# The gated activations of a decoder layer: transposed by VectorE in 32x32 squares instead of by TensorE

## The chip, the cores and the metric

The kernel runs on one core of a Trainium2 chip. The metric is device time in microseconds (us). Before the change it is 2656.92 us, the median of three runs (2655.61 to 2657.28). The engines are called by short names: PE is TensorE, DVE is VectorE, ACT is ScalarE, POOL is GpSimd, and SP is the engine whose queue issues most of the DMAs. PEld is the weight-load side of PE.

## The reference

The reference is one decoder layer on x of shape 16 x 112 x 1024 (1792 tokens) in float32. It has three blocks, each followed by a residual sum and a layer norm. Cut to the first block, which the change touches:

```python
s = silu(x @ w_gate.T)                 # 1792 x 2752
_, idx = top_k(-abs(s), 1376)          # the smaller half of each row ...
s[row, idx] = 0.0                      # ... is set to zero
h = s * (x @ w_up.T)
x = layernorm(x + h @ w_down.T)
```

The second block is cross attention over a context of 16 x 375 x 1024 (32 query heads, 8 key heads of 32), the third a linear layer with 4-bit weights. Neither is changed.

## The kernel before

The tokens are 14 tiles of 128. The work runs in stages on PE, one after the other.

- **Gates** (5.9 to 526 us): per tile six chunks of about 456 columns, eight products each (line 146). The results go through ACT and DVE to the DRAM buffer s_d.
- **Keys and values** (526 to 853 us): lines 176 and 184.
- **Up** (853 to 1403 us): per tile six chunks, 512, 512 and 352 columns twice, eight products each (line 234).
- **Down** (1405 to about 1890 us): h times w_down by a seven-product scheme over 2 x 2 blocks (line 546), with layer norm behind it.
- **Attention and the last layer**: the rest.

Beside the first three stages ACT and DVE look for the threshold of each row, which decides what is set to zero. For each tile there are 31 steps; in a step ACT counts over 1824 columns (line 284) and DVE over 928 (line 287), then DVE updates the candidate (lines 295 and 296). Two tiles are searched in turns. When a tile's search ends, `finish` adds twelve pieces: eight on DVE (lines 314 to 343), four on POOL (lines 347 and 348), and the mask goes to m_d. The function `beside`, called after each half step, takes one such piece and then emits chunks of the stream until it has emitted `share` columns more: the sum of the stream's weighted widths over 448 half steps. An up chunk is weighted 1.07 times its width.

Everything between is in the order in which it is written, on every engine: `as_written` ties each instruction to the one before it on its engine. So an instruction that waits holds all that is behind it on that engine, and a DMA that waits holds the DMAs behind it in the same queue.

An up chunk n goes through these steps. `emit` first calls `turn` for a chunk three back. Then `up_chunk(n)` calls `load_up(n + 1)`: on SP the tile's input uxT if chunk n + 1 is the first of a tile (line 138), then that chunk's s and mask (lines 211 and 212), and on POOL s times mask (line 213). Then come the eight products into a PSUM bank. Then `settle` emits the evacuation of the chunk before: DVE multiplies s by the product in PSUM (line 241), which gives h, 128 tokens on partitions. `turn` makes h transposed: PE transposes each 128 columns (line 255) into one of two PSUM banks, ACT copies them to the tile hT (lines 257 and 261), and POOL's queue stores hT in the DRAM buffer hT_d of that token tile (lines 258 and 262). The stream's products have the six other banks.

The down stage loads blocks of hT_d on SP (`block`, lines 532 and 533), 128 rows of h by 128 tokens for each of 11 parts, the last with 96 rows. Each part is the stationary operand of one product (`product`, line 546). DVE adds and subtracts whole blocks (`combine`, lines 553 and 554).

Of the kernel before, what the change touches and what calls it, by code (L numbers as in the profile page):

```python
# [10 lines left out]
F32 = mybir.dt.float32  # L11
# [6 lines left out]
ALU = mybir.AluOpType  # L18
AX = mybir.AxisListType
PSUM = bass.MemoryType.PSUM  # L20
DRAM = bass.MemoryType.DRAM

P = 128
B, S, D = 16, 112, 1024
NT = B * S
TT = NT // P
# [4 lines left out]
Q = 32  # L31
NKQ = -(-SK // Q)
SKP = NKQ * Q
NKP = -(-SK // P)
NH, NKV, HD = 32, 8, 32
REP = NH // NKV
KVD = NKV * HD
# [8 lines left out]
FH = FF // 2  # L46
UP_CHUNKS = [(h * FH + o, w) for h in range(2) for o, w in ((0, 512), (512, 512), (1024, 352))]
HK = -(-FH // P)
FULL, REST = FH // P, FH % P
# [48 lines left out]


def gates_keys_up(  # L100
    nc, tc, ident, xT, wg, wu, ctxT, wk, wv, s_d, m_d, hT_d, k_d, v_d, down, left, ps_g, ps_t
):


# [14 lines left out]
    io = io_ctx.enter_context(tc.tile_pool(name="g_io", bufs=2, side="right"))  # L119
# [103 lines left out]
    def up_chunk(n):  # L223
        t, c = ups[n]
        off, w = UP_CHUNKS[c]
        if n == 0:
            load_up(0)
            for tag, many, bufs in (("wk", 4, 1), ("wv", 4, 1), ("ctx", 6, 2), ("ctx", 6, 2)):
                to_load.extend(down.place(kvp, tag, many, bufs))
        load_up(n + 1)  # L230
        load_down()
        pu = ps_g.tile([P, 512], F32, tag="pg", name=f"pu_{t}_{c}")
        for kc in range(KC):
            nc.tensor.matmul(  # L234
                pu[:, :w], xts[t][:, kc, :], wu_sb[0][:, kc, ds(off, w)],
                start=(kc == 0), stop=(kc == KC - 1),
            )

        def evacuate():
            s = sm[t, c]  # L240
            nc.vector.tensor_mul(s[:, :w], s[:, :w], pu[:, :w])

        return evacuate

    def turn(n):

        t, c = ups[n]
        off, w = UP_CHUNKS[c]
        h = sm.pop((t, c))
        k0, nk = off // FH * HK + off % FH // P, -(-w // P)  # L250
        pt = ps_t.tile([P, 4, P], F32, tag="pt", name=f"pt_{t}_{c}")
        hT = io.tile([P, 4, P], F32, tag="hT", name=f"hT_{t}_{c}", bufs=2)
        for k in range(nk):
            r = min(P, w - k * P)
            nc.tensor.transpose(pt[:r, k, :], h[:, ds(k * P, r)], ident)  # L255
        whole = w // P
        nc.scalar.copy(hT[:, :whole, :], pt[:, :whole, :])
        nc.gpsimd.dma_start(hT_d[t][:, k0 : k0 + whole, :], hT[:, :whole, :])
        if nk > whole:
            r = w % P  # L260
            nc.scalar.copy(hT[:r, whole, :], pt[:r, whole, :])
            nc.gpsimd.dma_start(hT_d[t][:r, k0 + whole, :], hT[:r, whole, :])

    state = {}

# [100 lines left out]
    stream = deque()  # L366
# [6 lines left out]
    for b in range(B):  # L373
        for u in range(2 + NKP):
            stream.append((SK if u < 2 else KVD, lambda b=b, u=u: kv_unit(b, u)))
    for n, (t, c) in enumerate(ups):
        stream.append((UP_CHUNKS[c][1] * 1.07, lambda n=n: up_chunk(n)))
    found, pieces = set(), deque()


# [90 lines left out]
class Down:  # L471
# [54 lines left out]
    def block(self, t, h):  # L526

        pool = (self.a1, self.a2)[self.n_blocks // 4 % 2] if self.a2 else self.a1
        self.n_blocks += 1
        a = pool.tile([P, HK, P], F32, tag="h", name=f"h_{self.n_blocks}", bufs=4)  # L530
        h_d = self.hT_d[t]
        self.nc.sync.dma_start(a[:, :FULL, :], h_d[:, ds(h * HK, FULL), :])
        self.nc.sync.dma_start(a[:REST, FULL, :], h_d[:REST, h * HK + FULL, :])
        return a

    def first_blocks(self):
# [6 lines left out]
    def product(self, bank, a, b):  # L543
        for k in range(HK):
            r = P if k < FULL else REST
            self.nc.tensor.matmul(  # L546
                bank, a[:r, k, :], b(k)[:r],
                start=(k == 0), stop=(k == HK - 1),
            )

# [85 lines left out]
    def load_sums(self, j):  # L636

        v = self.nc.vector
        a11, a12, a21, a22 = (self.block(2 * j + i, h) for i in range(2) for h in range(2))
        self.combine(v, a22, a21, a22, ALU.add)  # L640
        self.combine(v, a21, a11, a21, ALU.subtract)
        self.combine(v, a22, a22, a11, ALU.subtract)
        self.combine(v, a12, a12, a22, ALU.subtract)
        self.live[j] = a22, a21, a12

    def load_rest(self, j):

        a21, a22 = (self.block(2 * j + 1, h) for h in range(2))
        self.combine(self.nc.vector, a21, a21, a22, ALU.add)
        self.live[j] = a21, a22  # L650

    def last_pass(self, beside):
# [119 lines left out]
def attention_and_ffn(nc, tc, ident, ident_b, negh, x1_d, k_d, v_d, queries, wf_sb, wo, out):  # L772
# [16 lines left out]
    with ExitStack() as ctx:  # L789
# [23 lines left out]
        def load_values(b, c):  # L813
            vals[b, c] = ld.tile([P, NKP, P], F32, tag="v", name=f"v_{b}_{c}")
            nc.sync.dma_start(
# [304 lines left out]
@with_exitstack  # L1120
def kernel(
    ctx: ExitStack,
    tc: tile.TileContext,
    x: bass.AP,
    xT: bass.AP,
    ctxT: bass.AP,
    wg: bass.AP,
    wu: bass.AP,
    wd: bass.AP,
    wq: bass.AP,  # L1130
    wk: bass.AP,
    wv: bass.AP,
    wo: bass.AP,
    qw: bass.AP,
    qs: bass.AP,
    qz: bass.AP,
    out: bass.AP,
):
    nc = tc.nc
    const = ctx.enter_context(tc.tile_pool(name="const", bufs=1))  # L1140
    dram = ctx.enter_context(tc.tile_pool(name="dram", bufs=1, space=DRAM))
    ident = const.tile([P, P], F32, tag="ident", name="ident")
    make_identity(nc, ident)
    ident_b = const.tile([P, P], BF16, tag="ident_b", name="ident_b")
    nc.vector.tensor_copy(ident_b, ident)
    negh = const.tile([P, 1], F32, tag="negh", name="negh")
    nc.gpsimd.memset(negh, -0.5)

    s_d = [dram.tile([P, FF], F32, tag=f"s{t}", name=f"s_d{t}") for t in range(TT)]
    m_d = [dram.tile([P, FF], BF16, tag=f"m{t}", name=f"m_d{t}") for t in range(TT)]  # L1150
    k_d = dram.tile([B, P, 2, SK], F32, tag="k", name="k_d")
    v_d = dram.tile([B, SKP, KVD], F32, tag="v", name="v_d")
    x1_d = dram.tile([NT, D], F32, tag="x1", name="x1_d")

    hT_d = [dram.tile([P, 2 * HK, P], F32, tag=f"h{t}", name=f"hT_d{t}") for t in range(TT)]
    with as_written(nc, tc):
        with ExitStack() as psum:
            ps_g = psum.enter_context(tc.tile_pool(name="ps_g", bufs=6, space=PSUM))
            ps_t = psum.enter_context(tc.tile_pool(name="ps_t", bufs=2, space=PSUM))
            with ExitStack() as left:  # L1160
                down = Down(nc, tc, negh, wd, hT_d, x, x1_d, ps_g)
                gates_keys_up(
                    nc, tc, ident, xT, wg, wu, ctxT, wk, wv, s_d, m_d, hT_d, k_d, v_d, down, left,
                    ps_g, ps_t,
                )
                down.first_passes()
                a_w = ctx.enter_context(tc.tile_pool(name="a_w", bufs=1, side="right"))
                wq_sb = a_w.tile([P, KC, D], F32, tag="wq", name="wq_sb")
                wf_sb = a_w.tile([P, 8, D], BF16, tag="wf", name="wf_sb")
                queries = Queries(nc, tc, ctx, ident, x1_d, wq_sb, lambda: down.bank("pq"))  # L1170
                with tc.tile_pool(name="q", bufs=2, side="right") as q_pool:

                    def load_wq(i):
                        nc.scalar.dma_start(wq_sb[:, :, ts(i, D // 4)], wq[:, :, ts(i, D // 4)])

                    loads, computes = unpack_steps(nc, q_pool, wf_sb, qw, qs, qz)
                    beside = [[] for _ in range(TT // 2)]
                    for i, j in enumerate((1, 1, 2, 3, 4, 4, 5, 6)):
                        beside[j].append(computes[i])
                    for i, j in enumerate((0, 0, 1, 1, 2, 3, 4, 4)):  # L1180
                        beside[j].append(loads[i])
                    for i in range(4):
                        beside[i // 2].append(lambda i=i: load_wq(i))
                    beside[4].append(lambda: queries.fetch(0, 0))
                    beside[5] += [lambda: queries.rows(0, 0), lambda: queries.fetch(0, 1)]
                    beside[6].append(lambda: queries.rows(0, 1))
                    down.last_pass(beside)
            for mc in range(EARLY):
                queries.chunk(0, mc)
        attention_and_ffn(nc, tc, ident, ident_b, negh, x1_d, k_d, v_d, queries, wf_sb, wo, out)  # L1190
# [48 lines left out]
```

## Time and profile before

| | before |
|---|---|
| median of three runs | 2656.92 us |
| the profiled execution | 2661.48 us |
| its span, first to last instruction | 2659.7 us |
| mean granted TensorE clock | 0.983 |
| PE busy | 2584.9 us (97%) |
| DVE busy | 1730.8 us (65%) |
| ACT busy | 1377.6 us (52%) |
| POOL busy | 1053.8 us (40%) |
| line 234, products of the up stage | 530.6 us, 1344 records |
| line 255, transposes by PE | 44.2 + 7.6 us, 308 records |
| lines 257 and 261, copies by ACT | 50.0 us, 112 |
| lines 258 and 262, stores by POOL | 112 issues |
| line 241, multiplies by DVE | 52.5 us, 84 |
| line 546, products of the down stage | 1078 |

The profile page shows busy time by engine, the span in 40 slices (a digit is the busy share in tenths), and the chain of work that ended last. A line of the timeline or of the chain begins with the start and the length in us. A group's line ends with busy time and mean ns of one, then the idle time of the engine ahead of it and what ended it. A line of waits names who waited, for whom, the total in us, how often, and the longest. The products are pipelined, so a record of a product is longer than the step from one to the next: 16 records of a 512-column chunk take 6.87 us on the chain, 0.43 us each, where a record shows 592 ns.

### The profile page before, as it was taken

How to read it: one execution, taken by the hardware profiler on the slowest of the kernel's cores; microseconds unless marked ns; L12 is line 12 of the kernel's file. 1: busy time of each engine (PE TensorE's matmuls, PEld its weight loads, DVE VectorE, ACT ScalarE, POOL GpSimd, SP SyncE). 2: the span in 40 equal slices, each digit the busy share in tenths (PEclk: the TensorE clock that was granted, in tenths of full speed). 3: DMA queues.
4: the chain of work that ended last, by engine and by line, in shares of the span. 5: the costliest groups of instructions: out<-in, count | busy, mean ns of one | idle time of the engine just before them, and what ended most of it. 6: DMA issues, size and time to landing. Idle time of an engine off the chain costs nothing.

```text
span 2659.7 us, 33179 instructions
## 1 busy us (share of the span) xinstructions
PE 2584.9 (97%) x10266; PEld 1482.7 (56%) x10266; DVE 1730.8 (65%) x3579; ACT 1377.6 (52%) x2413; POOL 1053.8 (40%) x1097
## 2 busy tenths in 40 slices
PE   9999999999999999999999999998899999999997
PEld 4444444577776555555554444443556666667663
DVE  0478778866876788788730343158467777777773
ACT  0487787777767777787610000000255555565553
POOL 0002022213322444344450000023277888788783
PEclk9999999999999999999999999999889999999998
DMA  6221223154443543443346222166567777777763
GB/s 253 94 74 56 77 91 126 51 195 168 181 169 136 162 140 121 143 132 117 95 145 228 86 96 94 59 204 202 133 169 196 196 191 193 192 205 194 188 175 103
DMA packets 216960, 387.70 MB, mean 146 GB/s; under 512 B 32080, under 2 KB 151120, under 8 KB 212688
## 3 DMA queue, kind: packets, MB, share of 16 engines
q1 hardware_dynamic: 165456, 257.19, 32.3%
q0 software_dynamic: 35840, 100.59, 11.6%
q10 hardware_dynamic: 15488, 27.80, 3.5%
q8 instruction: 83, 1.36, 0.2%
q14 instruction: 93, 0.76, 0.1%
HBM read 208.36 MB, written 76.43 MB: 107 GB/s over the span
## 4 chain that ended last, share of the span: by engine, by line
PE 90%; DVE 3%; DMA 3%; ACT 2%; issue 1%; POOL 1%; ACTq 0%; SPq 0%; POOLq 0%; DVEq 0%
PE pg L146 20%; PE pu L234 19%; PE m L546 14%; PE bank L924 7%; PE pk L184 6%; PE pk L176 6%; PE bank L765 6%; PE sc L832 4%; PE po L887 3%; PE bank L975 2%; PE pt L255 1%; ACT probs L840 1%; DVE b L727 1%; DMA xr<-x_d 1%; DVE nmax L838 1%
## 5 line engine op out<-in xcount | busy, mean ns | idle before, releaser
L284 ACT ACTIVATE ja<-a,cand 128x1824 int8<-128x1824 f32 x434 | 788.6, 1817 | 178.4 <-DVE cand L296 174.4
L287 DVE TENSOR_SCALAR_CACHE_REDUCE jv<-a,cand 128x928 uint8<-128x928 f32 x434 | 510.0, 1175 | 56.9 <-ACT a L271 48.8
L234 PE MATMUL pu<-wu_sb,uxT 128*128 128x512 f32 (+1 forms) x1344 | 530.6, 548 | 0.0
L146 PE MATMUL pg<-wg_sb,gxT 128*128 128x456 f32 (+1 forms) x1344 | 519.9, 550 | 5.9 <-DMA wg_sb<-in_wg_dram 5.9
L840 ACT ACTIVATE probs<-sc,nmax 128x375 f32<-128x375 f32 x512 | 287.4, 573 | 237.6 <-DVE nmax L838 218.2
L146 PEld LDWEIGHTS pg<-wg_sb,gxT 128*128 128x128 f32 x1344 | 256.2, 191 | 268.8 <-issue 265.3
L849 POOL TENSOR_TENSOR probs<-probs,sums 128x1500 f32<-128x1500 f32 x128 | 344.2, 2689 | 142.4 <-DVE sums L848 123.2
L234 PEld LDWEIGHTS pu<-wu_sb,uxT 128*128 128x128 f32 x1344 | 249.0, 190 | 230.0 <-issue 188.4
L838 DVE TENSOR_REDUCE nmax<-sc 128x2 f32<-128x750 f32 x256 | 228.6, 932 | 150.3 <-PE sc L832 150.2
L546 PE MATMUL m<-wd,h 128*128 128x512 f32 (+1 forms) x616 | 268.0, 597 | 0.0
L860 DVE STREAM_TRANSPOSE squares<-probs 128x1536 f32<-128x1536 f32 x128 | 224.0, 1750 | 9.7 <-DMA weights<-squares 5.5
L155 POOL DMA_DIRECT2D s_d<-s x84 | 46.0, 548 | 427.4 <-DVE s L154 351.5
L765 PE MATMUL bank<-x1T,wq_sb 128*128 128x224 f32 x976 | 202.6, 361 | 0.0
L546 PEld LDWEIGHTS m<-wd,h 128*128 128x128 f32 (+1 forms) x616 | 117.5, 191 | 149.2 <-issue 145.1
L765 PEld LDWEIGHTS bank<-x1T,wq_sb 128*128 128x128 f32 x976 | 181.3, 191 | 33.2 <-issue 30.2
L924 PE MATMUL bank<-wo_sb,aT 128*128 128x256 f32 x832 | 195.0, 388 | 0.0
L758 ACT COPY x1T<-pq 128x448 f32<-128x448 f32 x4 | 2.0, 535 | 371.6 <-PE pq L757 371.6
L874 POOL DMA_DIRECT2D weights<-squares x320 | 178.6, 564 | 9.0 <-issue 6.6
L924 PEld LDWEIGHTS bank<-wo_sb,aT 128*128 128x128 f32 x832 | 155.4, 192 | 46.5 <-issue 24.9
L184 PE MATMUL pk<-wv_sb,ctx 128*128 128x256 f32 (+1 forms) x768 | 168.4, 379 | 0.0
L176 PE MATMUL pk<-ctx,wk_sb 128*128 128x375 f32 x512 | 164.4, 478 | 0.0
L184 PEld LDWEIGHTS pk<-wv_sb,ctx 128*128 128x128 f32 (+1 forms) x768 | 144.0, 188 | 24.8
(118 smaller groups left out, 2881.8 us busy)
## 6 DMA issues: line engine op xcount, KB each, us to landing
weights<-squares SPq DMA_DIRECT2D x704, 96.0 KB, 3.3
h<-hT_d SPq DMA_DIRECT2D x56, 640.0 KB, 4.5
weights<-squares POOLq DMA_DIRECT2D x320, 96.0 KB, 3.4
ctx<-in_ctxT_dram SPq DMA_DIRECT2D x16, 1500.0 KB, 6.7
a<-s_d SPq DMA_DIRECT2D x14, 1376.0 KB, 7.9
us<-s_d SPq DMA_DIRECT2D x56, 256.0 KB, 2.7
hT_d<-hT POOLq DMA_DIRECT2D x56, 256.0 KB, 3.1
s_d<-s POOLq DMA_DIRECT2D x56, 228.0 KB, 2.2
```

The costliest lines, as they stand in the source:

```text
L146: nc.tensor.matmul(pg[:, :w], xts[t][:, kc, :], wg_sb[:, kc, ds(off, w)], start=(kc == 0), stop=(kc == KC - 1),)
L176: nc.tensor.matmul(pk[:, :SK], wk_sb[:, kc, ts(u, P)], c[:, kc, :], start=(kc == 0), stop=(kc == KC - 1),)
L184: nc.tensor.matmul(pk[:n, :KVD], c[:, kc, ds(at, n)], wv_sb[:, kc, :], start=(kc == 0), stop=(kc == KC - 1),)
L234: nc.tensor.matmul(pu[:, :w], xts[t][:, kc, :], wu_sb[0][:, kc, ds(off, w)], start=(kc == 0), stop=(kc == KC - 1),)
L284: nc.scalar.activation(ja, a[:, NV:], AF.Sign, bias=cand, scale=-1.0, accum_out=st["sgn"])
L287: nc.vector.tensor_scalar(jv, a[:, :NV], cand, -(TOPK - 1 - NA / 2), ALU.is_lt, ALU.add, accum_out=st["nlt"])
L546: self.nc.tensor.matmul(bank, a[:r, k, :], b(k)[:r], start=(k == 0), stop=(k == HK - 1),)
L765: nc.tensor.matmul(pq[:, :GT], self.wq_sb[:, kc, ts(mc, P)], self.x1T[g][:, kc, :], start=(kc == 0), stop=(kc == KC - 1),)
L838: nc.vector.tensor_reduce(nmax[h], sc[h][:, :, :SK], AX.X, ALU.max, negate=True)
L840: nc.scalar.activation(pr[:, i, :SK], sc[i // 2][:, i % 2, :SK], AF.Exp, bias=nmax[i // 2][:, i % 2 : i % 2 + 1], accum_out=sums[:, i : i ...
L849: nc.gpsimd.tensor_tensor(pr, pr, sums.unsqueeze(2).to_broadcast([P, 4, SK]), ALU.mult)
L924: nc.tensor.matmul(pp[:, :256], aT[:, h, r, :], wo_sb[:, h * REP + r, ts(i, 256)], start=(h == 0 and r == 0), stop=(h == 1 and r == REP - 1),)
```

## The change

`turn` no longer uses PE, ACT or the two PSUM banks. DVE transposes each chunk of h in squares of 32 x 32 from SBUF to SBUF. A square's transpose stays on its 32 partitions, so the block is not yet in order: the 32 tokens of group b lie on partitions 32 b to 32 b + 31. Four stores a chunk, one for each group, put it together in hT_d; two go on SP's queue and two on POOL's. Within a chunk the rows k of the four 128-column parts are innermost, so a row of 32 tokens by four parts is 512 bytes in DRAM (three parts and 384 bytes for the 352-column chunk, of which the missing 32 rows are set to zero by POOL).

The down stage loads a block in one transfer of 128 partitions. A part's stationary operand is now every fourth (third) word of it. The blocks' sums are made in one instruction over all columns, so lines 553 and 554 become one there. All eight PSUM banks go to the stream, and the weight of an up chunk in the pace is its width.

```diff
@@ turn
-        k0, nk = off // FH * HK + off % FH // P, -(-w // P)
-        pt = ps_t.tile([P, 4, P], F32, tag="pt", name=f"pt_{t}_{c}")
-        hT = io.tile([P, 4, P], F32, tag="hT", name=f"hT_{t}_{c}", bufs=2)
-        for k in range(nk):
-            r = min(P, w - k * P)
-            nc.tensor.transpose(pt[:r, k, :], h[:, ds(k * P, r)], ident)
-        whole = w // P
-        nc.scalar.copy(hT[:, :whole, :], pt[:, :whole, :])
-        nc.gpsimd.dma_start(hT_d[t][:, k0 : k0 + whole, :], hT[:, :whole, :])
+        at, whole, nk = off % FH, w // P, -(-w // P)
+        tile = io.tile([P, 512], F32, tag="hT", name=f"hsq_{t}_{c}", bufs=2)
+        sq = tile[:, : nk * P].rearrange("p (m f k) -> p m k f", m=SQ, k=nk)
+        nc.vector.transpose(
+            sq[:, :, :whole],
+            h[:, : whole * P].rearrange("p (k m f) -> p m k f", m=SQ, f=Q),
+        )
         if nk > whole:
-            r = w % P
-            nc.scalar.copy(hT[:r, whole, :], pt[:r, whole, :])
-            nc.gpsimd.dma_start(hT_d[t][:r, k0 + whole, :], hT[:r, whole, :])
+            n = w % P // Q
+            nc.gpsimd.memset(sq[:, n:, whole], 0.0)
+            nc.vector.transpose(
+                sq[:, :n, whole], h[:, whole * P : w].rearrange("p (m f) -> p m f", f=Q)
+            )
+        n = nk * Q
+        to = hT_d[t].rearrange("(m p) h n -> p m h n", p=Q)
+        for b in range(SQ):
+            queue = (nc.sync, nc.gpsimd)[b % 2]
+            queue.dma_start(
+                to[:, :, off // FH, ds(at + b * n, n)],
+                tile[ts(b, Q), : nk * P].rearrange("p (m n) -> p m n", m=SQ),
+            )
@@ the stream
-        stream.append((UP_CHUNKS[c][1] * 1.07, lambda n=n: up_chunk(n)))
+        stream.append((UP_CHUNKS[c][1], lambda n=n: up_chunk(n)))
@@ Down.block
-        a = pool.tile([P, HK, P], F32, tag="h", name=f"h_{self.n_blocks}", bufs=4)
-        h_d = self.hT_d[t]
-        self.nc.sync.dma_start(a[:, :FULL, :], h_d[:, ds(h * HK, FULL), :])
-        self.nc.sync.dma_start(a[:REST, FULL, :], h_d[:REST, h * HK + FULL, :])
+        a = pool.tile([P, HK * P], F32, tag="h", name=f"h_{self.n_blocks}", bufs=4)
+        self.nc.sync.dma_start(a, self.hT_d[t][:, h])
@@ Down.product
+            at, n = k // 4 * 4 * P, min(4, HK - k // 4 * 4)
             self.nc.tensor.matmul(
-                bank, a[:r, k, :], b(k)[:r],
+                bank, a[:r, ds(at + k - at // P, P, n)], b(k)[:r],
@@ Down.load_sums, and load_rest likewise
-        self.combine(v, a22, a21, a22, ALU.add)
+        v.tensor_tensor(a22, a21, a22, ALU.add)
...
@@ tile_decoder_kernel
-            ps_g = psum.enter_context(tc.tile_pool(name="ps_g", bufs=6, space=PSUM))
-            ps_t = psum.enter_context(tc.tile_pool(name="ps_t", bufs=2, space=PSUM))
+            ps_g = psum.enter_context(tc.tile_pool(name="ps_g", bufs=8, space=PSUM))
```

More of the change, by code (lines that the diff above doesn't have):

```diff
@@ L34 @@
 NKP = -(-SK // P)
+SQ = P // Q
 NH, NKV, HD = 32, 8, 32
@@ L100, in gates_keys_up @@
 def gates_keys_up(
-    nc, tc, ident, xT, wg, wu, ctxT, wk, wv, s_d, m_d, hT_d, k_d, v_d, down, left, ps_g, ps_t
+    nc, tc, xT, wg, wu, ctxT, wk, wv, s_d, m_d, hT_d, k_d, v_d, down, left, ps_g
 ):
@@ L639, in load_sums @@
         a11, a12, a21, a22 = (self.block(2 * j + i, h) for i in range(2) for h in range(2))
-        self.combine(v, a22, a21, a22, ALU.add)
-        self.combine(v, a21, a11, a21, ALU.subtract)
-        self.combine(v, a22, a22, a11, ALU.subtract)
-        self.combine(v, a12, a12, a22, ALU.subtract)
+        v.tensor_tensor(a22, a21, a22, ALU.add)
+        v.tensor_tensor(a21, a11, a21, ALU.subtract)
+        v.tensor_tensor(a22, a22, a11, ALU.subtract)
+        v.tensor_tensor(a12, a12, a22, ALU.subtract)
         self.live[j] = a22, a21, a12
@@ L648, in load_rest @@
         a21, a22 = (self.block(2 * j + 1, h) for h in range(2))
-        self.combine(self.nc.vector, a21, a21, a22, ALU.add)
+        self.nc.vector.tensor_tensor(a21, a21, a22, ALU.add)
         self.live[j] = a21, a22
@@ L1153 @@
     x1_d = dram.tile([NT, D], F32, tag="x1", name="x1_d")
-    hT_d = [dram.tile([P, 2 * HK, P], F32, tag=f"h{t}", name=f"hT_d{t}") for t in range(TT)]
+    hT_d = [
+        dram.tile([P, 2, HK * P], F32, tag=f"h{t}", name=f"hT_d{t}") for t in range(TT)
+    ]
     with as_written(nc, tc):
         with ExitStack() as psum:
-            ps_g = psum.enter_context(tc.tile_pool(name="ps_g", bufs=6, space=PSUM))
-            ps_t = psum.enter_context(tc.tile_pool(name="ps_t", bufs=2, space=PSUM))
+            ps_g = psum.enter_context(tc.tile_pool(name="ps_g", bufs=8, space=PSUM))
             with ExitStack() as left:
@@ L1162 @@
                 gates_keys_up(
-                    nc, tc, ident, xT, wg, wu, ctxT, wk, wv, s_d, m_d, hT_d, k_d, v_d, down, left,
-                    ps_g, ps_t,
+                    nc, tc, xT, wg, wu, ctxT, wk, wv, s_d, m_d, hT_d, k_d, v_d, down, left, ps_g,
                 )
```

## The prediction, made before the changed kernel was run

> **What bounds the kernel now.** I read the page first, then the chain of waits in order of time, the groups by form, and last the waits and the timeline of the stage that the change touches (the up stage, 853 to 1403 us).
>
> ```profile
> PE   9999999999999999999999999998899999999997
> DVE  0478778866876788788730343158467777777773
> ...
> PE 90%; DVE 3%; DMA 3%; ACT 2%; issue 1%; POOL 1%; ACTq 0%; SPq 0%; POOLq 0%; DVEq 0%
> ```
>
> TensorE (PE) is at nine tenths or more nearly throughout, and 90% of the chain is its own work. So what leaves PE in the up stage can leave the total, unless something else then ends last. The chain through two chunks at a tile's end, beside VectorE (DVE) and the SP queue in the same microseconds:
>
> ```profile
> 1107.86 0.44 PE pt L255 x4
> 1108.30 6.87 PE pu L234 x16
> 1115.17 0.44 PE pt L255 x4
> 1115.61 6.87 PE pu L234 x16
> 1122.48 0.33 PE pt L255 x3
> 1122.80 4.74 PE pu L234 x16
> 1127.54 0.44 PE pt L255 x4
> 1127.98 6.87 PE pu L234 x16
> ```
> ```profile
> 1130.39 0.66 DVE L241 TENSOR_TENSOR us<-us,pu 128x512 f32<-128x512 f32 x1
> ```
> ```profile
> 1116.48 0.42 SPq L138 DMA_DIRECT2D uxT<-in_xT_dram  x1
> ```
>
> PE runs chunk after chunk without a gap; the transposes of line 255 stand between. DVE, which also runs the threshold search, is behind: the chunk that PE ended at 1122.48 is multiplied at 1130.39, 7.9 us later. SP does not care: it issued the next tile's input (uxT) at 1116.48, 11.5 us before PE used it at 1127.98. What SP waits for in this stage, and what DVE does:
>
> ```profile
> SPq L211 <- PE pt L255: 387.9, 76, 6.4
> ```
> ```profile
> ACT ja L284 <- DVE cand L296: 71.5, 54, 3.2
> DVE us L241 <- PE pu L234: 67.7, 32, 6.8
> ```
>
> SP is held by PE's transposes 76 times, so it keeps step with PE. DVE waits for PE in only 32 of 84 multiplies: in the others it is the late one.
>
> **The change, part by part.**
>
> *Transposes off PE.* Three chunks carry 0.44 + 0.44 + 0.33 = 1.21 us of them on the chain; 84 chunks are 28 such triples: **-34 us**, all on the path.
>
> *Copies off ACT.* Lines 257 and 261: 32.4 + 10.2 + 7.4 = 50 us, off the path (ACT waits for DVE and PE). It shortens the search's ACT side by half a microsecond a chunk.
>
> *Squares on DVE.* The nearest row is the attention's own transpose by squares:
>
> ```profile
> L860 DVE STREAM_TRANSPOSE squares<-probs 128x1536 f32<-128x1536 f32 x128 | 224.0, 1750 | 9.7 <-DMA weights<-squares 5.5 <-POOL probs L849 3.9 <-issue 0.2
> ```
>
> 1750 ns for 1536 columns is 1.14 ns a column: 0.58 us for 512, and 0.29 + 0.11 for the short chunk's 256 + 96; with a fixed part in each I take 0.62 and 0.56. 56 x 0.62 + 28 x 0.56 = 50 us. But that row writes runs of 32 neighbours, and the change writes every fourth word. Here a rule speaks against it: the Trainium skill (Advanced Engine Details and Errata, Memory Cachelines) says SBUF lines are 16 bytes and that accesses that each fall on another line are penalised. Four rows innermost are exactly 16 bytes. By the row a chunk of 512 costs 0.62 us, by the rule perhaps twice (my estimate, 1.15 us, or 30 us more over 56 chunks). No instruction of DVE in this trace steps that far; I take the row and keep the rule for the range. The same step comes into line 546's weight loads:
>
> ```profile
> L546 PEld LDWEIGHTS m<-wd,h 128*128 128x128 f32 x560 | 106.8, 191 | 135.8 <-issue 132.2 <-DVE h L553 2.4 <-DMA b<-in_wd_dram 0.7
> L975 PEld LDWEIGHTS <-x2T 128*128 128x128 bf16 x224 | 21.9, 103 | 40.2 <-ACT x2T L969 12.7 <-issue 6.9
> L968 PEld LDWEIGHTS <-xb 128*128 128x128 bf16 x112 | 9.4, 150 | 8.5 <-DVE xb L961 6.2 <-issue 0.8 <-DVE x L929 0.4
> ```
>
> Line 968 reads bf16 at a 16-byte step in 150 ns, line 975 without a step in 103. In that ratio 191 ns become 280. A pass of 512 columns lasts 430 ns (6.87 / 16) and the next load runs under it, so 0; if it took over 430 ns, each ns costs 1.08 us over the 1078 loads.
>
> *Does DVE still keep up?* From 853 to 1290 it is busy 357 of 437 us, 66 chunks. The squares add 66 x 0.6 = 40, and PE would want the same work in 437 - 66 x 0.4 = 411 us: 397 of 411, nearly full. The pace is written in columns: before, 92,732 weighted columns over 448 steps of the search are 207 a step, at 13.42 ns (6.87 / 512) 2.78 us; without the factor 1.07 it is 90,384 / 448 = 201.8 and 2.71 us. So DVE gets a shorter step and more work in it.
>
> *SP moved behind DVE.* This is where I expect the gain to go. Two of four stores a chunk are put on SP ahead of load_up's loads. They wait for the squares on DVE. Queued behind them are the next tile's uxT, then s and the mask. The squares of chunk n-4 stand on DVE directly ahead of the multiply of n-2; uxT of a tile that starts with n comes behind them. In the lines above: chunk 42 starts at 1127.98 and its uxT was issued at 1116.48; with the change it can be issued only after the squares ahead of the multiply at 1130.39. The prices: squares of a short chunk 0.56, a semaphore 0.1, two issues of a 32-row store and the load itself.
>
> ```profile
> L874 SPq DMA_DIRECT2D weights<-squares x704: 585/600/1882, 1927.3 to 2615.3; - x176
> ...
> DMA to landing us min/median/max: 2.1/3.3/8.0
> ```
> ```profile
> L138 SPq DMA_DIRECT2D uxT<-in_xT_dram x13: 419/424/1754, 880.9 to 1352.6; - x13
> ...
> DMA to landing us min/median/max: 3.8/4.9/5.7
> ```
>
> 0.56 + 0.1 + 2 x 0.60 + 4.9 = 6.8 us from the start of the squares to the landing; PE has one short chunk, 4.74 us, to cover it. So PE stands 2.0 us at a tile's start if the squares begin just as PE ends the fifth chunk, lag + 1.4 if DVE lags (the lag is that of the multiply, 0.56 later), and about 0.9 if DVE came early and waited.
>
> The lag of the fifth chunk's multiply behind PE at the 13 tile changes, read as above: 2.3, 0.1, 5.3, 0.1, 6.7, 0.1, 7.9, 2.9, 1.2, 2.1, 0.2, 4.3, 0.2. It rises each time a search ends: lines 314 to 343 then put some 15 us of extra work on DVE (43 + 24 + 24 + 97 + 16 + 4 us over 14 tiles) within three chunks, and it takes about six more to work off. Five such bursts lie in the stage; their lag at the next change is 5.3 on average (5.3, 6.7, 7.9, 2.1, 4.3). Squares (+0.6) and a faster PE (+0.4) against a relieved ACT (-0.5) let it grow by some 0.5 a chunk over four chunks: 7.3 + 1.4 = 8.7 a burst, 44 us; the first change 2.3 + 1.4 = 4; seven quiet ones 0.9 each, 6. **+54 us**. From below (no growth, landings at 3.8): 5 x 5.6 = 28. From above (growth of 4, quiet ones 2): 5 x 10.7 + 14 + 4 = 72.
>
> *Clock.* A stall of 8 us may lower PE's clock: in the window 1820 to 1870, with PE busy 31 of 50 us, the granted clock was 0.84. I take 1 us for each of five: **+5**, between 0 and 15.
>
> *Entry of the down stage.* The first h loads, at 1392.0 before, come behind the squares of chunk 80: about 1.5 us after PE ends chunk 82, 4.5 and more to land, against 4.74 of cover: **+2**, less the transposes at the very end, in the 34 already.
>
> *With one answer.* Eight banks for six: the skill (Perfetto Trace Analysis, Matmul Optimizations) asks for all eight, which would promise a gain; PE's idle time before line 234 is 0.0, so by the row it is 0. POOL: 168 stores for 112 at 0.56 and 28 memsets at 0.4 (line 192) are +42 us on an engine busy 245 of 550; its mask pieces can hold a store, and then squares two chunks on. DMA: 512-byte packets took 29 ns and 2 KB ones from POOL 133, so four for one is even. The h blocks load in one transfer for two and 35 small DVE additions of 280 ns go, both where DVE waits for PE: 0.
>
> Sum: -34 + 54 + 5 + 2 = **+27**, rounded to +25 as the quiet changes may hide. The profiled execution took 2661.5 us (span 2659.7 and 1.8 around it), 4.6 above the median; from the median 2656.9 + 25 gives **2682**.
>
> **Rivals.**
> 1. *The gain stays (0.20).* DVE, with ACT relieved, works its lag off before the tile changes, or uxT lands in 3.8. Then 13 x 0.9 = 12 of stalls stand against 34: 2635. For it: DVE still idles 80 of 437 us. Against: the lags of 5 to 8. It decides where the stalls at 13 changes average below 2.6 us (34 / 13).
> 2. *Both cancel (0.10).* Stalls near the lower bound, 28 + 5: within 5 us of 2657.
> 3. *Strided writes bind DVE too (0.15).* 1.15 us a chunk: lag grows 0.5 a chunk faster, 5 x 2.5 and about 3 at the quiet changes: 2697, up to 2725.
> 4. *Weight loads stick out (0.05).* At 500 ns, 70 x 1.08 = 75: over 2730.
>
> **Numbers.** The likeliest case (0.50) is 2682, its own range 2664 to 2706. The range of 8 in 10 reaches to the gain that stays and to the strided writes: 2638 to 2712, leaving about half of the first rival below and the weight loads with the end of the third above. Repeats differ by 0.06%, so 0.2% (5 us) is about what can be told from none. Faster 0.20; same 0.10; slower 0.50 + 0.15 + 0.05 = 0.70.
>
> **What would show it.** Right: PE idle before line 234, released by the uxT load, some 50 us at tile starts; SP's wait for DVE's squares in place of line 255; uxT issued under 6 us ahead of use. Squares near 0.6 us (row) or 1.15 (rule); weight loads of line 546 under 430 ns with PE gapless there. Wrong: no idle before line 234 and the down stage starting near 1370, or PE waiting for a bank behind DVE's multiplies instead.

## The result and the profile after

The changed kernel takes **2737.59 us** (median of four, 2734.65 to 2740.34) where the kernel before takes 2657.1 beside it: 1.0302 of the time, interval 1.0284 to 1.0319. It is slower by 80 us; forecast were 25, and the top of the range was 2712. The profiled execution took 2734.65 us, its span is 2732.9.

The page of the kernel after (slices of PE and of its granted clock, then the chain's shares):

```profile
PE   9999999999999897898959999999788999999996
...
PEclk9999999999999998999979999999898999999998
...
PE 74%; DVE 10%; DMA 5%; POOL 3%; issue 3%; ACT 3%; SPq 1%; ACTq 1%; DVEq 0%; POOLq 0%
```

Slices 13 to 22 hold the up stage. PE, at nine before, now has eights, a seven and a five there, and its clock falls in the two worst of these slices, the 16th and the 21st. Before, 90% of the chain was PE; now 74%, and the rest went to DVE, DMA and POOL, none of which should set the end in a stage of matrix products. The costliest groups say who waits:

```profile
L235 PE MATMUL pu<-wu_sb,uxT 128*128 128x512 f32 (+1 forms) x1344 | 539.9, 565 | 84.2 <-DMA uxT<-in_xT_dram 42.9
...
L557 PEld LDWEIGHTS m<-wd,h 128*128 128x128 f32 (+1 forms) x616 | 180.2, 293 | 86.4 <-issue 31.4
```

Line 235 is the old 234, the products of the up stage: PE stood 84.2 us ahead of them, half of it put down to the load of uxT. Line 557 is the old 546: its weight loads take 293 ns on average, not 191 (308 where the words are 16 bytes apart, 250 where they are 12). In the kernel before, line 234 had no idle time, and the down stage began at 1404.69:

```profile
L234 PE MATMUL pu<-wu_sb,uxT 128*128 128x512 f32 (+1 forms) x1344 | 530.6, 548 | 0.0
...
1404.69 359.15 PE m L546 x836
```

The longest pieces of the chain after, in order of time, at the end of the up stage:

```profile
1383.96 16.27 PE pu L235 x32
1432.12 4.77 DMA uxT<-in_xT_dram
1437.03 40.22 PE pu L235 x96
1477.25 368.43 PE m L557 x858
```

A landing of uxT, issued too late, stands on the chain ahead of the last tile. The down stage begins at 1477.25 where it began at 1404.69; from there to the end of the span it is 1255.7 us for 1255.0 before. **All of the loss, 73 us between the two profiled spans, is in the up stage.** (The other 7 us to the medians' difference: the profiled execution before was 4.4 above its median, the one after 2.9 below.) The down stage runs as before: 368.43 / 858 is 0.43 us a product.

From the weight loads of line 235 I read where PE stood: only ahead of a tile's first chunk. The 13 tile changes show 4.2, 5.3, 5.3, 0, 19.6, 0, 9.0, 0, 4.6, 6.9, 0, 19.2 and 14.1 us, together 88. At each of the nine stalls PE starts 0.1 us after uxT has landed, also where the profile names another engine: uxT is what ended all nine. The chunks behind a stall run slower, 18 us in all (the chunk behind the stall of 19.2 took 8.8 us for 6.9). The stage before and after, with the granted clock in the third column from the end:

```profile
853.00:1403.00 550.00, 550.00 (x1645) 284.25 (x1644) 418.50 (x1033) 367.95 (x449) 245.29 (x256) 1.00 0.42 134
```
```profile
853.00:1477.00 624.00, 539.76 (x1346) 262.56 (x1345) 461.55 (x1110) 319.25 (x331) 268.69 (x340) 0.92 0.41 118
```

A mean of 0.92 over 624 us is about 50 us of full clock not granted. Most of that lies inside the stalls, where PE has nothing to do; the 18 us are what falls on products. Without stalls and slower running, PE needs 56 x 6.87 + 28 x 4.74 = 517 us; 517 + 88 + 18 = 623, and the stage lasts from 853 to 1477.

What SP waits for in the up stage of the kernel after:

```profile
SPq L270 <- DVE hsq L263: 166.8, 27, 13.2
SPq L270 <- DVE hsq L256: 122.8, 29, 13.7
SPq L270 <- DVE us L242: 92.0, 18, 13.1
SPq L270 <- POOL hsq L262: 52.3, 7, 16.5
```

The first three are the forecast: the stores (270) held by the squares (256, 263), or by the multiply ahead of them (242). The fourth is not in it. Line 262 is the memset of 32 words a partition that clears the pad of the short chunk. It takes 0.16 us, and SP waited up to 16.5 us for it. The timeline of POOL at the largest stall:

```profile
1061.99 0.86 POOL L214 TENSOR_TENSOR us<-us,um 128x352 f32<-128x352 f32 x1
1062.80 1.49 POOL L358 TENSOR_TENSOR e<-e,c 128x688 bf16<-128x688 bf16 x1
1064.36 1.49 POOL L359 TENSOR_TENSOR m<-m,e 128x688 bf16<-128x688 bf16 x1
1065.81 1.48 POOL L358 TENSOR_TENSOR e<-e,c 128x688 bf16<-128x688 bf16 x1
1067.37 1.49 POOL L359 TENSOR_TENSOR m<-m,e 128x688 bf16<-128x688 bf16 x1
1069.15 0.60 POOL L361 DMA_DIRECT2D m_d<-m  x1 [0.30 <-POOL m L359]
1069.74 0.16 POOL L262 MEMSET hsq<- 128x32 f32 x1
```

DVE had the squares of the same chunk done ten microseconds before the memset:

```profile
1059.21 0.52 DVE L256 STREAM_TRANSPOSE hsq<-us 128x256 f32<-128x256 f32 x1
1059.62 0.25 DVE L263 STREAM_TRANSPOSE hsq<-us 128x96 f32<-128x96 f32 x1
```

SP's queue, and then PE:

```profile
1055.29 0.39 SPq L213 DMA_DIRECT2D um<-m_d  x1
1069.93 1.16 SPq L270 DMA_DIRECT2D hT_d<-hsq  x2
1071.18 0.92 SPq L139 DMA_DIRECT2D uxT<-in_xT_dram  x1
```
```profile
1076.73 7.69 PE L235 MATMUL pu<-wu_sb,uxT 128*128 128x512 f32 x12 [19.14 <-DMA uxT<-in_xT_dram]
```

Read from the bottom: PE stands for 19 us for uxT; uxT stands behind two stores on SP; they stand for the memset; and the memset stands behind the mask pieces of a search that has just ended. The squares had been ready since 1059.9.

### The profile page after: what moved, and what is told of

It is laid out like the page before. It is cut to its first block, busy times and chain, and to the rows that moved or that the text cites. A ratio compares the mean times of both kernels' runs of the same rounds, so it can differ in the third digit from the quotient of the medians.

```text
span 2732.9 us, 32604 instructions
## 1 busy us (share of the span) xinstructions
PE 2566.6 (94%) x9944; PEld 1567.9 (57%) x9958; DVE 1790.0 (65%) x3656; ACT 1334.3 (49%) x2301; POOL 1074.3 (39%) x1181
## 3 DMA queue, kind: packets, MB, share of 16 engines
q0 software_dynamic: 34496, 90.96, 10.8%
## 4 chain that ended last, share of the span: by engine, by line
PE 74%; DVE 10%; DMA 5%; POOL 3%; issue 3%; ACT 3%; SPq 1%; ACTq 1%; DVEq 0%; POOLq 0%
PE pg L147 19%; PE m L557 14%; PE pu L235 9%; PE bank L935 6%; PE pk L177 6%; PE pk L185 5%; PE bank L776 5%; PE sc L843 4%; PE po L898 3%; DVE jv L298 3%; PE bank L986 2%; POOL e L358 1%; ACT probs L851 1%; DMA xr<-x_d 1%; POOL m L359 1%
## 5 line engine op out<-in xcount | busy, mean ns | idle before, releaser
L235 PE MATMUL pu<-wu_sb,uxT 128*128 128x512 f32 (+1 forms) x1344 | 539.9, 565 | 84.2 <-DMA uxT<-in_xT_dram 42.9
L235 PEld LDWEIGHTS pu<-wu_sb,uxT 128*128 128x128 f32 x1344 | 262.5, 196 | 361.4 <-issue 252.5
L557 PEld LDWEIGHTS m<-wd,h 128*128 128x128 f32 (+1 forms) x616 | 180.2, 293 | 86.4 <-issue 31.4
L214 POOL TENSOR_TENSOR us<-us,um 128x512 f32<-128x512 f32 (+1 forms) x84 | 89.3, 1064 | 195.3 <-DMA um<-m_d 195.0
```

Source lines behind the costliest of these rows:

```text
L235: nc.tensor.matmul(pu[:, :w], xts[t][:, kc, :], wu_sb[0][:, kc, ds(off, w)], start=(kc == 0), stop=(kc == KC - 1),)
L557: self.nc.tensor.matmul(bank, a[:r, ds(at + k - at // P, P, n)], b(k)[:r], start=(k == 0), stop=(k == HK - 1),)
```

## The experiments

Each kernel is the changed one with the edit shown, or the one before where that is said. The kernel with the earlier load counts its lines two higher. Times are medians, ratios are to the kernel before with 95% intervals; "gaps" and "slower" are PE's stalls and the slower running behind them, read as above (88 and 18 in the changed kernel).

**1. The load of uxT, four chunks earlier.**

```diff
-        if c == 0:
-            load_x(t, "u")
+        if n == 0:
+            load_x(0, "u")
+        if c == 2 and t + 1 < TT:
+            load_x(t + 1, "u")
```

> The changed kernel, with the next tile's uxT loaded four chunks earlier (ahead of the stores that wait for the squares). My theory (uxT queued on SP behind DVE's squares costs the time): the idle time of PE at tile starts (88 us in the changed kernel) and the half clock behind it (18 us) go; 2640 to 2665 us. Rival A (the squares, at 1.1 us with a 16-byte step, make DVE the bound): PE waits elsewhere instead, for banks, and the time stays over 2700. Rival B (POOL's memset, held by the mask pieces, is what delays the stores and all loads behind them): s and mask come late too, DVE waits for POOL in its multiplies, 2680 to 2710.

Measured: 2673.14 us, 1.0050 (1.0035 to 1.0065), 64 us less than the changed kernel. The gaps fall from 88 to 14, the slower running from 18 to 5. So the stalls do come through the place of uxT in SP's queue. But 2673 lies between my range and that of rival B, and the kernel is still not faster than before, though its PE does 33 us less. Who waits now, on PE and then on SP:

```profile
PE m L559 <- DMA h<-hT_d: 21.1, 1, 21.1
```
```profile
SPq L272 <- POOL hsq L264: 74.6, 16, 17.6
```

PE runs ahead of DVE, up to 30 us at the last tile, and pays once at the entry of the down stage: the first h blocks are loaded from hT_d by the same SP queue, behind the last stores. SP now waits 75 us for the memset, for 52, which is what rival B had named.

**2 and 3. The two suspects of the size: strided writes, and the memset.** In the first, squares are written in runs of 32 neighbours, so the tokens come in another order; the sizes, the stores and all the instructions are the same.

```diff
-        sq = tile[:, : nk * P].rearrange("p (m f k) -> p m k f", m=SQ, k=nk)
+        sq = tile[:, : nk * P].rearrange("p (m k f) -> p m k f", m=SQ, k=nk)
```

> The changed kernel, with the squares written in runs of 32 neighbours in place of every fourth word; the stores and loads keep their shapes, so the tokens land in another order and the output isn't the reference's. My theory: a square of 512 columns falls from 1.1 to 0.6 us, PE's stalls at tile starts shrink by the smaller lag only, to 55 to 75 us: 2695 to 2720. Rival A (DVE bound by the strided writes): most of the loss comes back, under 2670. Rival B: 2715 or more.

The second lets DVE clear the pad:

```diff
-            nc.gpsimd.memset(sq[:, n:, whole], 0.0)
+            nc.vector.memset(sq[:, n:, whole], 0.0)
```

> The changed kernel, with the missing 32 rows of a short chunk zeroed by DVE in place of POOL. My theory with the memset as a part of it: SP's waits for the memset (52 us) go, the three stalls of 14 to 20 us at tile starts become 5 to 10: 2695 to 2715. Rival A: no change beyond 5 us. Rival B: the bulk of the stalls goes, under 2680.

Measured: runs of 32 give 2727.03 us, 1.0257 (1.0240 to 1.0274), 10.6 less than the changed kernel; gaps 81, slower 14. My 2695 to 2720 was missed, on the side of rival B. The pad on DVE gives 2689.19, 1.0110 (1.0095 to 1.0125), **48.4 less**, more than I had expected of it; gaps 47, slower 13. One engine's name on an instruction of 0.16 us is worth 48 us. The chain of this kernel at the tile change shown above:

```profile
1054.70 0.28 DVE hsq L263
1055.00 0.32 SPq L270
1055.37 0.42 SPq L270
1055.91 3.91 DMA uxT<-in_xT_dram
1059.82 0.14 issue
1059.96 24.38 PE pu L235 x55
```

This is the chain that the forecast worked out: squares, two stores, the load, PE. It lasts 5.3 us from the start of the second squares; POOL is not in it. The three largest stalls, 19.6, 19.2 and 14.1, become 7.7, 10.8 and 0.0 here, which is 34 of the 41 us by which the gaps fall; two more, 5.3 and 6.9, lose 3.5 each.

**4. Both together: what the forecast had assumed.**

> The changed kernel with the pad zeroed by DVE and the squares in runs of 32 neighbours (so the output isn't the reference's), the stores and loads as they are: what the prediction assumed, squares of 0.62 us and no hold by the memset. If the prediction's step for SP (54 us of stalls, 5 of clock, against 34 saved) was sized right, 2672 to 2692. If SP's order costs less than I took and the rest was squares and memset, 2640 to 2670.

Measured: 2682.32 us, 1.0095 (1.0078 to 1.0112); gaps 41.5, slower 12. The up stage ends at 1424.5, 20 us after that of the kernel before, for 25 forecast. The groups of DVE by form, in the changed kernel:

```profile
L256 DVE STREAM_TRANSPOSE hsq<-us 128x512 f32<-128x512 f32 x56 | 61.8, 1106 | 22.9 <-DMA hT_d<-hsq 22.4 <-issue 0.3
L256 DVE STREAM_TRANSPOSE hsq<-us 128x256 f32<-128x256 f32 x28 | 14.7, 526 | 11.3 <-DMA hT_d<-hsq 11.3
L263 DVE STREAM_TRANSPOSE hsq<-us 128x96 f32<-128x96 f32 x28 | 7.1, 253 | 0.0
```

and in this one:

```profile
L256 DVE STREAM_TRANSPOSE hsq<-us 128x512 f32<-128x512 f32 x56 | 39.4, 706 | 23.6 <-DMA hT_d<-hsq 23.5
L256 DVE STREAM_TRANSPOSE hsq<-us 128x256 f32<-128x256 f32 x28 | 12.4, 441 | 13.8 <-DMA hT_d<-hsq 11.9 <-DMA wd<-in_wd_dram 1.8
L263 DVE STREAM_TRANSPOSE hsq<-us 128x96 f32<-128x96 f32 x28 | 6.8, 243 | 0.0
```

Writing every fourth word costs 1106 ns for 706, and DVE is busy 83.6 us with the squares for 58.6. On the total that is 11 us where POOL clears the pad, and 7 where DVE does (2689.2 to 2682.3; here the intervals of the two ratios overlap, but the profiled executions agree: stalls and slower running are 61 us in one and 54 in the other). The memset is 45 us with runs of 32 (2727.0 to 2682.3) and 48 without.

**5. The queue alone, without any squares.** The kernel before, with its stores put on SP's queue and the transposes left on PE:

```diff
-        nc.gpsimd.dma_start(hT_d[t][:, k0 : k0 + whole, :], hT[:, :whole, :])
+        nc.sync.dma_start(hT_d[t][:, k0 : k0 + whole, :], hT[:, :whole, :])
...
-            nc.gpsimd.dma_start(hT_d[t][:r, k0 + whole, :], hT[:r, whole, :])
+            nc.sync.dma_start(hT_d[t][:r, k0 + whole, :], hT[:r, whole, :])
```

> The kernel before, transposes by PE and copies by ACT, with one thing of the change: the stores of the transposed tile on SP's queue, ahead of load_up's loads, in place of POOL's. Theory (what costs is uxT behind a store that waits for the search's engines): PE waits for uxT at tile starts, 15 to 60 us slower, 2672 to 2717. Rival (it takes the squares on DVE to do harm): within 8 us of before.

Measured: 2697.98 us, 1.0148 (1.0131 to 1.0166), 40 us more than before. SP waits in its up stage:

```profile
SPq L258 <- ACT hT L257: 263.1, 51, 23.3
SPq L258 <- ACT hT L261: 153.3, 27, 9.6
```

and PE:

```profile
PE pu L234 <- DMA uxT<-in_xT_dram: 23.2, 7, 4.7
```

At all 13 tile changes PE now starts 0.05 us after uxT has landed. The stalls read from the weight loads are 26 us and the slower running 8, together the 35 us by which the up stage ends later than before, at 1439.5. So the stalls need neither DVE's squares nor strided writes. It is enough that stores which wait stand ahead of the loads in the queue; ACT's copies cause them as well, though less than half as much as the changed kernel.

**6 to 8. Is the gain of 34 us there?** The early load with runs of 32, with the pad on DVE, and with the first h blocks on another queue.

> The changed kernel with both: uxT four chunks earlier and squares written in runs of 32 neighbours (so the output isn't the reference's). My theory: PE never waits in the up stage, 34 us of transposes are gone: 2620 to 2635. Compared with the run that only loads uxT early it tells what the strided writes cost once uxT is no bound: under 10 us by my theory, 40 or more by rival A. Rival B: no faster than 2670.

> The changed kernel with uxT loaded four chunks earlier and the pad zeroed by DVE. Theory as it now stands (two separate holds: uxT behind the squares on SP, and the stores behind POOL's memset, which the mask pieces hold): with uxT early the memset still makes the squares wait for the stores of two chunks back (68 us of DVE in the run that only loads uxT early); that falls under 35, and the time to 2645 to 2663. Rival (the memset only mattered because uxT stood behind it): as with uxT early alone, 2668 to 2676.

Measured: early load with runs 2661.22, 1.0012 (1.0003 to 1.0020), 12 us less than the early load alone but far from my 2620 to 2635; early load with the pad on DVE 2656.44, 0.9995 (0.9986 to 1.0004), gaps 6, slower 1. The memset is thus worth 17 us even when uxT is loaded ahead of the stores (2673.1 to 2656.4). In both, PE still stands some 20 us at the entry of the down stage (19.6 and 19.5). DVE's wait for the stores of a square buffer, expected under 35 us in the second, is 56: there I was wrong, the memset was not the main thing behind it. The third sends the first three h blocks through ACT's queue:

```diff
-        self.ahead = deque(self.block(2 * j, h) for j, h in self.order[:3])
+        self.ahead = deque(self.block(2 * j, h, self.nc.scalar) for j, h in self.order[:3])
...
-    def block(self, t, h):
+    def block(self, t, h, queue=None):
...
-        self.nc.sync.dma_start(a, self.hT_d[t][:, h])
+        (queue or self.nc.sync).dma_start(a, self.hT_d[t][:, h])
```

> As the run before, and the three first blocks of h for the down stage loaded on ACT's queue, which is idle then, in place of SP's. Theory: PE's wait of 21 us at the entry of the down stage (SP held by the last stores) goes: 12 to 22 us less than the run before, 2625 to 2650. Rival (DVE's lag at the end holds the banks that the down stage needs): less than 5 us gained.

Measured: 2639.50, 0.9935 (0.9918 to 0.9952). The wait at the entry falls from 19.5 to 2.5, and the time by 16.9. Another wait on the same queue, at another place.

**9 to 11. A third square buffer, and then what is left of the other parts.**

```diff
-        tile = io.tile([P, 512], F32, tag="hT", name=f"hsq_{t}_{c}", bufs=2)
+        tile = io.tile([P, 512], F32, tag="hT", name=f"hsq_{t}_{c}", bufs=3)
```

> As the run before, with three buffers for the squares in place of two. Theory: the waits of the squares for the stores go from DVE; as PE has no wait in the up stage left, the time changes by under 5 us. Rival (DVE is now the bound of the up stage): 10 us or more are gained.

Measured: **2629.53 us, 0.9896 (0.9881 to 0.9911)**, 28 us less than the kernel before and 108 less than the changed one. The chain of its up and down stages has no gap worth the name:

```profile
853.77 364.61 PE pu L237 x944
...
1372.44 368.79 PE m L559 x858
```

The up stage ends at 1372.4, 32 us ahead of the kernel before. My own figure for the third buffer, under 5 us, was too low: it gave 10. I had taken PE to be without a wait, but in the run before it still stood 5.8 and 1.7 us at two tile changes; with three buffers 0.9 us is left. DVE's waits in that stage:

```profile
DVE us L244 <- POOL us L216: 45.1, 12, 20.3
...
DVE hsq L258 <- DMA hT_d<-hsq: 2.6, 3, 1.2
```

The squares no longer wait for their stores (2.6 us for 56); the multiplies wait for POOL instead, which costs nothing here, because PE has banks and inputs in hand while DVE runs up to some 31 us behind. On this kernel, runs of 32 and six banks for eight:

> The fastest version so far (uxT early, pad on DVE, first h on ACT's queue, three buffers) with the squares in runs of 32 neighbours (so the output isn't the reference's). PE is without a gap there, while DVE's lag grows to 32 us over the stage. Theory: the strided squares are hidden by the lead of PE: within 4 us of that version, with a lag under 15 us at the end. Rival: they are on the path there too: 8 us or more faster.

```diff
-            ps_g = psum.enter_context(tc.tile_pool(name="ps_g", bufs=8, space=PSUM))
+            ps_g = psum.enter_context(tc.tile_pool(name="ps_g", bufs=6, space=PSUM))
```

> The fastest version so far, with six banks for the stream in place of eight. Theory: PE's lead is up to five chunks only near the end, so six banks cost 0 to 6 us. Rival (the banks carry the gain): 10 us or more slower.

Measured: 2629.19 (0.9891, 0.9876 to 0.9906) and 2629.79 (0.9895, 0.9880 to 0.9910): neither differs from 2629.53. With DVE off the path, its strided writes cost nothing; its largest lag falls from some 31 to 19 us, and it is 5 at the last chunk. The two banks cost nothing either.

**12. The pace alone.** The kernel before with the weight 1.07 of an up chunk taken away.

> The kernel before with one part of the change alone: the weight of an up chunk in the pace is its width, without the factor 1.07. Theory: the pace is worth little, 2652 to 2666, as DVE's lag stays under what PE's transposes allow. Rival (the pace alone overloads the search's steps and makes PE wait): over 2675.

Measured: 2658.14, 1.0003 (0.9996 to 1.0010). Worth nothing by itself.

## Why the prediction was wrong

The likeliest case had the direction right, and the wait that it named (uxT behind DVE's squares on SP) is there; the size is not, and one step that was put at nothing carries most of the miss.

| step of the prediction | forecast, us | shown, us |
|---|---|---|
| transposes off PE | -34 | -33: the up stage of the kernel without gaps lasts 518.7, before 551.4 |
| uxT behind DVE's squares, stalls | +54 | 41.5 with runs of 32 and no memset on POOL; 88 as changed |
| clock behind the stalls | +5 | 12 there; 18 as changed |
| POOL: "its mask pieces can hold a store, and then squares two chunks on" | 0 | +48, or +45 with runs of 32 |
| squares by the row of the attention, not by the rule | 50 busy | 84 busy, 59 in runs of 32; the step is +7 to +12 on the time |
| entry of the down stage | +2 | under 1 while PE is late; 20 once it is not |
| weight loads of line 546 | 0, 280 ns | 0, 308 ns at the 16-byte step, 293 on average |
| pace, banks | 0 | 0 each |

**The step that failed is POOL.** The sentence in the table names the right instructions and then gives them no price. I followed POOL's own stores, and looked for a delay two chunks on. I did not ask who waits for the new memset: the two stores of SP read the same tile, so they wait for POOL too, and uxT waits behind them. The forecast had put a price on SP behind DVE but counted the memsets only as busy time, 28 at 0.4 us. The price is not the instruction's 0.16 us but what stands ahead of it on POOL: the mask pieces of a finished search, eight instructions of 1.49 us, 12 us in all (the last four are in the timeline above). At two of the three largest stalls, the 5th and the 12th change, this comes on top of a burst of the search on DVE: with the pad on DVE 7.7 and 10.8 us remain there. At the 13th nothing remains: its 14.1 us are the memset's alone.

The delay "two chunks on" is there too, and had no price either. At the 10th change POOL's stores stand behind mask pieces, and DVE's squares behind those stores:

```profile
1279.76 1.12 POOL L270 DMA_DIRECT2D hT_d<-hsq  x2
```
```profile
1283.35 0.52 DVE L256 STREAM_TRANSPOSE hsq<-us 128x256 f32<-128x256 f32 x1 [4.93 <-DMA hT_d<-hsq]
```

At the 3rd change it is the same, with 4.19 us. In the up stage DVE waits 31.5 us for stores of the squares in the changed kernel, and still 30.9 with the pad on DVE. So the 41.5 us of stalls that are left with both undone are not DVE's search alone; how much of them is POOL's, no run separates.

**The squares** were the second step. The nearest row had the right operation and the wrong step of the write. The rule of the Trainium skill (Advanced Engine Details and Errata, Memory Cachelines), that accesses which each fall on another line are penalised, agrees with the trace: 1.106 us for 512 columns written at a step of 16 bytes, for 0.706 in runs. That my estimate of 1.15 us came so near is partly luck: I doubled 0.58 us, and it is 0.706 times 1.57. The row was also read too low, 0.62 us for the 0.706 of runs, since short squares carry more of a fixed part than I gave them (441 ns for 256 columns, 706 for 512). That rival was worth 7 to 12 us on the time, less than the 15 that I gave it, and alone stays inside the range: the run with the pad on DVE has the strided squares and takes 2689. So the two steps leave 80 - 48 - 7 = 25.

With both undone the kernel takes 2682.32 us, where 2682 was forecast. That agreement is in part luck, as it is better than its parts. The stalls were 41.5 for 54: a store's issue took about 0.4 us on SP for the 0.60 taken and uxT landed in 3.8 for 4.9, which is 1.5 us a change, or some 13 over the nine changes at which PE stood more than 0.4 us (my estimate). They also stood elsewhere: 5.9 and 4.0 us at the 2nd and the 9th change, which were to be quiet, and 0.5 at the 3rd, which was to be a burst. The clock cost 12 for 5: I took 1 us for each of five stalls, and it was 2.1 us at each of six. The parts of the trace add up to 20 us and not 25 in the profiled execution, which was 4 us under its own median. The quiet changes, 0.9 each by forecast, are often 0 (four of thirteen in the changed kernel).

**The rivals.** The gain that stays needed stalls below 2.6 us at a change: they were 6.8 on average. The saving on PE is there, though, and the fastest version shows it: 28 of the 34 us remain when the loads are taken from behind the stores, DVE clears the pad, and the squares have a third buffer. The weight loads that stick out would have given over 2730, near the time measured, but by another mechanism: they stayed under the 430 ns of a pass, and the down stage has no gap. The number alone would have pointed to the wrong part.

**Left open.** The three largest stalls were followed back to the memset instruction by instruction. For the two that lose 3.5 us each with the pad on DVE, the traces show squares that wait for POOL's stores, but not why the loss is 3.5. Not tried was the changed kernel with all its stores off SP's queue. The slower running behind a stall has a size (1.2 to 2.7 us after each of the nine stalls of 4.2 to 19.6 us in the changed kernel, no more after the long ones), but the runs give no rule for it.

## What to carry to other kernels

When a DMA is put in a queue ahead of others, list for every tile that it reads the last writer on each engine, however short, and what stands ahead of that writer on its engine: the queue takes over the worst of these lags, and hands it to all loads behind. Loads on which PE depends belong ahead of stores that wait, or on another queue: here the load four chunks earlier was worth 64 us, and another queue for the first h blocks a further 17. When work is taken from the engine that bounds, the engines behind it may need buffers for the lag that they now show: the third square buffer gave the last 10 us.

## What the runs showed of the hardware

- A transpose by DVE in 32 x 32 squares of 512 float32 columns takes 1106 ns when its output steps by 16 bytes, 706 in runs of 32 words. With a step of 12 bytes (256 columns) it is 526 for 441.
- Weight loads of float32, 128 x 128, take 308 ns at a 16-byte step and 250 at a 12-byte step, for 191 without one, and stay hidden under passes of 430 ns.
- PE pays for a gap twice: after each of nine stalls of 4.2 to 19.6 us (88 together) it lost another 1.2 to 2.7 us to slower running (18 together); the granted clock over the stage, stalls included, was 0.92.
- A 32-row store of 512-byte pieces is issued in 0.39 us on SP, and in 0.55 us on POOL.
